# A two-layer decoder kernel: products of the identity put ahead of TensorE's expected waits

## The chip, the cores and the metric

The kernel runs on one core of one Trainium2 chip. The metric is the device time of one execution in microseconds (us). TensorE (PE, with its weight loads shown apart as PEld), VectorE (DVE), ScalarE (ACT), GpSimd (POOL) and SyncE (SP, which issues the DMAs) each work through a list of instructions of their own, in order, and wait for each other by semaphores.

## The reference

Two decoder layers on 8 sequences of 256 tokens with 512 features, all in float32. Each of the six stages adds its result to `x` and normalises:

```python
x = _layernorm(x + L0_attn(x))                 # power attention: 16 query, 8 key heads of 128, (qk)^2, gated decay, causal
x = _layernorm(x + L0_xattn(x, ctx, ctx))      # 16 heads of 32 over 256 context tokens, causal
x = _layernorm(x + L0_ffn(x))                  # router over 128 experts, top 4, eight shared bases, a shared expert
x = _layernorm(x + L1_attn(x))                 # 32 query heads of 16, 8 key heads, softmax, and a memory read
x = _layernorm(x + L1_xattn(x, ctx, mask))     # 16 heads of 32, queries and output in int8 steps
x = _layernorm(x + L1_ffn(x))                  # 8 experts, top 2
```

## The kernel before

**Work.** The 2048 tokens are held as four groups `g` of 512 tokens (two sequences each), all stages in one launch, stage after stage with overlaps. A float32 product is made of three products in the type fp32r, of a high and a low part of each operand (`mm3`, lines 665 to 667: high by high, high by low, low by high). ScalarE or GpSimd rounds a tile to its high part and VectorE subtracts to get the low part (`split_ps`, `split_w`; lines 635, 636, 640, 641). Results of TensorE go to banks of PSUM, which come from six rings of buffers: `w` and `v` of two, `z`, `y`, `mm` and `m2` of one (printed as `m`). `Ctx.bank` (line 624) gives out the next buffer of a ring; a step that asks for one cannot write it before the last reader of the buffer's former content is done.

**Steps.** The program is a list of some thousand small steps (`proj`, `scores`, `probs`, `turn` and so on), each with a planned time. `Plan.record` builds a draft of the whole program and notes which instructions each step issues. `listed` then plays the draft: it holds a time for each engine (`free`), a duration for every instruction by its form (`occupied`), the end of every instruction (`end`), and chooses again and again, from the steps whose planned time lies within a window, the one that could start first. The result is one order of steps. `Plan.run` issues the steps of the real program in this order, and ties the instructions of each engine to it. So each engine's list is fixed by the played times, not by what happens on the chip.

**Constants.** `Ctx` makes the 128x128 identity in two types, `ident` in float32 and `identr` in fp32r (lines 584 to 587). Transposes on TensorE use them; a transpose writes its bank as a product does.

**Names that the prediction uses.** At the start, `values.proj` of the first stage multiplies the first tokens (`axth`, `axtl`) by the value and gate weights (`wvh`, `wvl`); its inputs come by DMA and are split first. Near 1676 us, at the start of the fourth stage, `memory_out` multiplies the memory's two parts `mh`, `ml` with elements of the queries (`m<-mh,sh`), `scores` gives `w<-k,q`, VectorE takes maxima `nm` of them (line 2029), and the maxima are turned by products with `identr` (`max_turn`, line 1141, shown as `m<-identr,ns` on the helper's line 658). At 1987 us SP issues the loads of the fifth stage's constants, `bqc` among them (line 2211). Line 1021 turns sums of the first stage in 32x32 blocks, line 1673 (`counts`) multiplies the router's turned exponentials `et`, 128 columns of weights, with a table of only 10 columns, line 2329 turns probabilities of the fifth stage. The last microseconds are the last stage (`l1_ffn`) on the last tokens, step after step, with little beside it.

The run of the steps, before:

```python
for k, n in enumerate(order or range(len(steps))):
    m = len(ins)
    steps[n].f()
```

## Time and profile before

| | |
|---|---|
| time, median of 3 runs | 2397.93 us (2394.85 to 2399.33) |
| the profiled execution: its own time | 2399.13 us |
| its span, first to last instruction | 2397.4 us |
| mean granted clock of TensorE | 0.958 |
| TensorE products: busy, number | 2191.5 us, 12779 |
| TensorE weight loads: busy, number | 1670.0 us, 12800 |
| VectorE, ScalarE, GpSimd busy | 1506.3, 1094.0, 718.0 us |
| mean DMA rate | 95 GB/s |

Busy time of TensorE counts a product from its start to its modelled end. Products overlap, so the pace, from one start to the next, is shorter than a product's duration: a product of 128x512 takes some 395 ns and the next starts some 230 ns later. The granted clock is the share of its full clock that TensorE is given; in this profile it is 1 or 0.5. A row of the timeline gives start (us), time (us), engine, line, operation, what is written from what, weights, shape and type, number, and in brackets the idle time before it and what ended it. A row of the windows view gives the stretch, then the busy time and number of instructions of PE, PEld, DVE, ACT and POOL, the granted clock, the DMA share and GB/s.

### The profile page before, as it was taken

The numbers are of one execution on the slowest core, as the hardware profiler recorded it, in microseconds if no ns is written. First come the engines' busy times: TensorE is split into PE (matmuls) and PEld (weight loads), VectorE is DVE, ScalarE is ACT, GpSimd is POOL, SyncE is SP. The second block draws the span as 40 slices with busy tenths as digits, with TensorE's granted clock in tenths as the row PEclk, the third lists the DMA queues.
The fourth block names the chain that finished last, engine by engine and source line by source line (L and its number), as shares of the span: only waits on it lengthen the run. The fifth ranks groups of instructions, "written<-read, shape, count | busy, mean of one in ns | idle before, by whom it ended". The sixth has DMA issues, their size and how long they took to land.

```text
span 2397.4 us, 36873 instructions
## 1 busy us (share of the span) xinstructions
PE 2191.5 (91%) x12779; PEld 1670.0 (70%) x12800; DVE 1506.3 (63%) x3563; ACT 1094.0 (46%) x2697; POOL 718.0 (30%) x978
## 2 busy tenths in 40 slices
PE   7999999899999689988989999998999997878885
PEld 5888877688887567666778778886556564546663
DVE  5655666656556655555655554444777876778885
ACT  3443444444444565654211321112456554678884
POOL 3544444544444211111112201001112323523233
PEclk9999999999999899998999999999799998899997
DMA  4111122112112777752563201103454353765630
GB/s 141 49 40 45 58 76 71 45 57 80 40 36 84 201 215 206 205 167 80 56 147 119 69 33 53 36 1 98 84 93 87 79 92 78 172 157 141 177 80 36
DMA packets 146266, 226.83 MB, mean 95 GB/s; under 512 B 23680, under 2 KB 46848, under 8 KB 145824
## 3 DMA queue, kind: packets, MB, share of 16 engines
q1 hardware_dynamic: 146080, 224.48, 36.0%
q8 instruction: 102, 1.67, 0.3%
q14 instruction: 84, 0.69, 0.1%
HBM read 162.43 MB, written 57.79 MB: 92 GB/s over the span
## 4 chain that ended last, share of the span: by engine, by line
PE 65%; DVE 14%; DMA 7%; ACT 7%; issue 4%; POOL 2%; SPq 1%; ACTq 0%; DVEq 0%; POOLq 0%
PE v L665 5%; PE v L667 5%; PE v L666 5%; PE w L667 3%; PE w L665 3%; PE w L666 3%; PE mm L652 3%; PE mm L665 3%; PE mm L667 3%; PE mm L666 3%; PE z L665 2%; PE z L667 2%; PE z L666 2%; PE w L652 2%; PE z L652 2%
## 5 line engine op out<-in xcount | busy, mean ns | idle before, releaser
L1038 POOL TENSOR_TENSOR x<-x,ot 128x512 f32<-128x512 f32 x128 | 171.7, 1341 | 261.3 <-ACT ot L1037 199.8
L2029 DVE TENSOR_REDUCE nm<-w 128x2 f32<-128x512 f32 x256 | 166.1, 684 | 44.7 <-PE w L652 44.2
L2072 ACT ACTIVATE pr<-v 128x512 f32<-128x512 f32 x256 | 139.4, 595 | 81.3 <-PE v L652 80.7
L1701 ACT ACTIVATE sg<-w 128x512 f32<-128x512 f32 x64 | 38.1, 598 | 258.1 <-PE w L667 245.7
L1037 ACT ACTIVATE ot<-m,rn 128x512 f32<-128x512 f32 x128 | 88.0, 687 | 79.6 <-PE m L667 76.7
L2329 PE MATMUL w<-ident,pr 128*128 128x128 f32 x512 | 97.1, 297 | 27.3 <-ACT pr L2315 21.2
L1352 ACT ACTIVATE pr<-w,nm 128x128 f32<-128x128 f32 (+1 forms) x256 | 105.3, 425 | 27.9 <-DVE nm L1345 12.2
L1034 DVE SCALAR_TENSOR_TENSOR x<-mm,rn,x 128x512 f32<-128x512 f32 x128 | 95.3, 745 | 31.1 <-PE mm L667 30.1
L665 PE MATMUL w<-wgh,ph 128*128 128x512 f32 x256 | 102.1, 399 | 2.7 <-ACT sg L1701 2.7
L666 PE MATMUL w<-wgl,ph 128*128 128x512 f32 x256 | 101.2, 395 | 3.4 <-DVE wgl L1591 3.4
L2329 PEld LDWEIGHTS w<-ident,pr 128*128 128x128 f32 x512 | 61.0, 146 | 59.6 <-ACT pr L2315 54.9
L1345 DVE TENSOR_REDUCE nm<-w 128x1 f32<-128x128 f32 (+1 forms) x256 | 77.4, 347 | 39.5 <-PE w L1340 29.5
L667 PE MATMUL w<-wgh,pl 128*128 128x512 f32 x256 | 101.2, 395 | 0.0
L1410 POOL TENSOR_TENSOR x<-x,oo 128x256 f32<-128x256 f32 x32 | 24.7, 773 | 240.5 <-DVE oo L1406 240.5
L1590 POOL TENSOR_SCALAR wgh<-raw 128x512 fp32r<-128x512 f32 x40 | 26.1, 654 | 226.1 <-PE w L667 182.8
L1704 DVE TENSOR_TENSOR sg<-sg,v 128x512 f32<-128x512 f32 x42 | 28.8, 686 | 97.8 <-PE v L667 87.7
L636 DVE TENSOR_TENSOR yl<-y,yh 128x512 fp32r<-128x512 f32 x64 | 44.0, 688 | 70.3 <-ACT yh L635 70.3
L635 ACT ACTIVATE yh<-y 128x512 fp32r<-128x512 f32 x64 | 38.2, 597 | 108.8 <-PE y L667 106.1
L978 DVE TENSOR_TENSOR a<-w,se 128x512 f32<-128x512 f32 (+1 forms) x128 | 67.5, 549 | 21.6 <-PE w L667 19.0
L986 ACT ACTIVATE a<-a 128x768 f32<-128x768 f32 x64 | 54.0, 844 | 55.9 <-DVE a L978 55.9
L2115 POOL TENSOR_TENSOR x<-x,oo 128x256 f32<-128x256 f32 x32 | 23.4, 730 | 185.7 <-DVE oo L2104 148.3
L994 DVE TENSOR_TENSOR al<-a,ah 128x768 fp32r<-128x768 f32 x64 | 69.2, 1083 | 13.8 <-POOL ah L990 13.5
(609 smaller groups left out, 7227.2 us busy)
## 6 DMA issues: line engine op xcount, KB each, us to landing
q<-rs SPq DMA_DIRECT2D x90, 128.0 KB, 3.5
b_pair<-rs SPq DMA_DIRECT2D x42, 256.0 KB, 5.6
q<-rs SPq DMA_DIRECT2D x36, 256.0 KB, 4.2
k<-ke SPq DMA_DIRECT2D x36, 256.0 KB, 6.1
raw<-in_Wq_dram SPq DMA_DIRECT2D x32, 256.0 KB, 2.7
eb<-lg SPq DMA_DIRECT2D x32, 256.0 KB, 3.5
raw<-in_Wc_dram SPq DMA_DIRECT2D x32, 256.0 KB, 3.4
raw<-in_L_ffn_w_gate_dram SPq DMA_DIRECT2D x32, 256.0 KB, 4.0
```

Of the source, the lines that this page charges most:

```text
L652: ins = self.K.nc.tensor.matmul(*args, **kw)
L665: nc.tensor.matmul(ps, lh, rh, start=first, stop=False)
L666: nc.tensor.matmul(ps, lh, rl, start=False, stop=False)
L667: nc.tensor.matmul(ps, ll, rh, start=False, stop=last)
L1034: nc.vector.scalar_tensor_tensor(xt, st["o", r], c, xt, ALU.mult, ALU.add)
L1037: nc.scalar.activation(ot, st["o", r], AF.Copy, scale=c)
L1038: nc.gpsimd.tensor_tensor(xt, xt, ot, ALU.add)
L1345: nc.vector.tensor_reduce(m[:, t : t + 1], st["w", j][:, t, : (t + 1) * P], AX.X, ALU.max, negate=True)
L1352: nc.scalar.activation(p_[:, t * P : (2 * t + 1) * P], st["w", j][:, t, : (t + 1) * P], AF.Exp, bias=st["m", j][:, t : t + 1], accum_out=s ...
L2029: nc.vector.tensor_reduce(st["nm"][:, :, h], st["w", h], AX.X, ALU.max, negate=True)
L2072: nc.scalar.activation(st["p", h], st["w", h], AF.Exp, scale=SCALE)
L2329: ins = nc.tensor.transpose(v[:, sb, t * P : (t + 1) * P], st["p", j][:, t, sb * P : (sb + 1) * P], K.ident)
```

## The change

While `listed` plays the order, it now also looks at the first instruction of a step, where that is TensorE's and the step allots buffers. It takes the time from when TensorE is free to when the inputs that other engines make are ready (`gap`), subtracts `GAP` = 0.3 us, and notes a number of spare products for the step: `SHARE` = 0.55 of the rest, at 0.06 us for one, 60 at most. `Plan.run` hands the number to the step, and the first call of `bank` in it issues so many products of `identr` by `identr` into the buffer that it has just allotted. The step's own product then writes the same buffer with its accumulation started anew, so nothing of them is kept. Each of these products is an fp32r product of its own with its weight load: up to 128 weight columns (as many as the buffer has rows) and up to 128 columns streamed. The draft has no such products, so the played times, and with them the order of the steps, are the same as before.

```diff
--- before.py
+++ after.py
@@ -38,6 +38,7 @@
 ST_E, FI_E, DF_E = 0.0, 5.9, 3.9
 
 SB, W_A, W_B, W_C, WC, WDD = -3000, 26.2, 23.9, 17.8, -5, -30
+GAP, SHARE = 0.3, 0.55
 LP, LA, LV = 0.325, 0.235, 0.215
 SE, WINDOW, SLACK, QL_D, ML_D, W_D, QX_D, TP = -350.0, 35.5, 0.033, 20, 14, 22.8, 0, 10
 
@@ -292,6 +293,7 @@
 
     def __init__(self, tc):
         self.tc, self.steps, self.last, self.strict, self.step = tc, [], {}, 1e9, None
+        self.spare = 0
 
     def at(self, t, raw, f, *args):
         self.steps.append((t, raw, len(self.steps), partial(f, *args)))
@@ -309,11 +311,11 @@
             s.ins = list(ins[n:])
         return self
 
-    def run(self, order=None, first=0):
+    def run(self, order=None, first=0, spare={}):
         steps = self.sorted()
         ins = self.tc.nc.cur_bb.bb.instructions
         for k, n in enumerate(order or range(len(steps))):
-            m = len(ins)
+            m, self.spare = len(ins), spare.get(n, 0)
             steps[n].f()
             for i in ins[m:]:
                 e = str(i.engine)
@@ -397,7 +399,7 @@
     turns, rings, ready, floors = {}, {}, {}, {}
     left = {name: {s for s in u if s.n >= first} for name, u in users.items()}
     last_use = {}
-    order = list(range(first))
+    order, spare = list(range(first)), {}
     for s in steps[first:]:
         f = s.f.func
         stage, *_, name = f.__qualname__.split(".")
@@ -467,6 +469,9 @@
         stop = t
         for n, i, before in s.pred:
             e = str(i.engine).split(".")[-1]
+            if e == "PE" and i is s.pred[0][1] and s.allocs:
+                gap = max([0.0, *(end[j] for j in before)]) - free[e]
+                spare[s.n] = min(60, max(0, int((gap - GAP) * SHARE / 0.06)))
             occ, lat, mode_ = occupied(i, mode)
             t = max([free.get(e, 0.0), *(end[j] for j in before)])
             t = max([t, *(ready.get(v.bass_ap.tensor.name, 0.0) for v in i.outs if hasattr(v, "bass_ap"))])
@@ -489,7 +494,7 @@
         todo.remove(s)
         order.append(s.n)
     K.played = max(end.values())
-    return order, first
+    return order, first, spare
 
 
 class Phase:
@@ -627,7 +632,16 @@
             n = self.turns[tag] = self.turns.get(tag, -1) + 1
             tag = TURNS[tag][n % len(TURNS[tag])]
         self.bufs[tag] = RINGS[tag]
-        return self.noted(self.psum.tile(list(shape), dt, tag=tag, name=tag, bufs=RINGS[tag]), RINGS[tag], None, ring)
+        t = self.psum.tile(list(shape), dt, tag=tag, name=tag, bufs=RINGS[tag])
+
+        part = t
+        while len(part.shape) > 2:
+            part = part[:, 0]
+        n = min(P, part.shape[1])
+        for _ in range(self.plan.spare):
+            self.nc.tensor.matmul(f32(part[:, :n]), self.identr[:, : part.shape[0]], self.identr[:, :n], start=True, stop=True)
+        self.plan.spare = 0
+        return self.noted(t, RINGS[tag], None, ring)
 
     def split_ps(self, hi, lo, ps):
 
@@ -2613,8 +2627,7 @@
     same = [nc.dram_tensor(f"{'out' if a is args[-1] else 'in'}{i}", a.shape, a.dtype, kind="ExternalOutput" if a is args[-1] else "ExternalInput").ap() for i, a in enumerate(args)]
     draft = planned(ctx, tile.TileContext(nc).__enter__(), *same)
     draft.plan.record()
-    order, first = listed(draft, draft.start, draft.window, SLACK)
-    planned(ctx, tc, *args).plan.run(order, first)
+    planned(ctx, tc, *args).plan.run(*listed(draft, draft.start, draft.window, SLACK))
 
 
 def planned(ctx, tc, x, x_turned, ctx_2048, ctx_turned, mask, *weights_and_out):
```

## The prediction

> **What bounds the kernel now.** I read the page first (busy time, chain), then the windows view on the grid at which the clock changes, then the timeline at the places where products are added. The page:

> ```profile
> PE 2191.5 (91%) x12779; PEld 1670.0 (70%) x12800; DVE 1506.3 (63%) x3563; ACT 1094.0 (46%) x2697; POOL 718.0 (30%) x978
> ...
> PE 65%; DVE 14%; DMA 7%; ACT 7%; issue 4%; POOL 2%; SPq 1%; ACTq 0%; DVEq 0%; POOLq 0%
> ```

> TensorE sets the end: 65% of the chain, and idle for only 206 us of 2397.4. Time can come back in two ways: a wait ends sooner, or the products behind it run at the full clock. The mean granted clock is 0.958. The stretches at half clock all begin and end on one grid of 3.41 us, as in these windows (columns: window and length; busy us of PE, PEld, DVE, ACT, POOL with counts; granted clock; DMA share; GB/s):

> ```profile
> 2151.10:2154.51 3.41, 1.87 (x15) 1.37 (x14) 3.31 (x14) 3.20 (x11) 1.27 (x1) 1.00 0.23 72
> 2154.51:2157.93 3.42, 3.10 (x17) 2.14 (x19) 2.33 (x10) 3.26 (x11) 1.38 (x4) 0.50 0.08 16
> 2157.93:2161.34 3.41, 3.41 (x25) 2.37 (x18) 1.23 (x6) 2.26 (x9) 0.00 (x0) 0.50 0.96 219
> 2304.70:2308.11 3.41, 2.20 (x14) 1.62 (x15) 2.58 (x14) 3.41 (x12) 0.00 (x0) 1.00 0.90 217
> 2308.11:2311.53 3.42, 3.42 (x26) 1.82 (x23) 1.82 (x5) 2.28 (x10) 0.00 (x0) 0.50 0.00 0
> ```

> A window in which PE is busy for some 55 to 65% is followed by one at half clock, and a full window, or nearly, is needed to leave it. The start is at half clock too, whatever the clock column says there (it has no event before 14.36): products of 264 columns start 0.22 us apart until 14.4 and 0.12 us apart after:

> ```profile
> 13.72 0.42 PE L665 MATMUL z<-wvh,axth 128*128 128x264 f32 x1
> 13.94 0.42 PE L666 MATMUL z<-wvl,axth 128*128 128x264 f32 x1
> ...
> 14.74 0.28 PE L665 MATMUL v<-wvh,axth 128*128 128x264 f32 x1
> 14.86 0.28 PE L666 MATMUL v<-wvl,axth 128*128 128x264 f32 x1
> ```

> **What is added.** The order of steps is played on the draft, which has no extra products, so every engine keeps its order. Comparing the built programs, only TensorE's list differs: 401 products at 40 places. Their sizes are uneven: 60 at the start, 28 and 47 near 802 and 806 us, 15 near 820, 39 near 1678, 60 (16 weight columns) near 1989, 19 and 15 near 2371 and 2384; the other 32 places hold 1 to 9 each. TensorE works its list in order, so each one is free only as far as it lies in a wait that exists on the chip. The first of a place takes over the wait for its bank's last reader from the step's own product; no wait is new, and what is queued behind is TensorE's own list.

> **What one costs.** The code counts 0.06 us each. No row shows a 128-column fp32r product behind a full 128x128 load. Where only 10 columns follow such a load, eight products start within 0.81 us (1137.63 to 1138.44): about 0.11 us each, set by the load. With 128 columns streamed (0.12 x 128/264 = 0.06 us) the load still sets the pace, so I take 0.11 at full clock; bounds 0.06 and 0.12. At half clock the stream alone is 0.22 x 128/264 = 0.107, the lower bound. I take 0.215, because loads slow with the clock too. The short transposes of L1021 show it, four of them in 0.43 us (pace 0.06) against 0.63 (pace 0.11):

> ```profile
> 59.90 0.43 PE L1021 MATMUL m<-ident,nr 32*128 32x32 f32 x4
> 441.92 0.63 PE L1021 MATMUL m<-ident,nr 32*128 32x32 f32 x4
> ```

> [...]

> The same figures say what the products do to the clock: they stream 0.053 us in 0.11, so the array works half of the time. That is enough to lift a window that just failed (60% busy), and too little, I think, to leave half clock, which here took windows that were nearly full. [...] Here windows that were half busy lowered it, so I do not count on half-busy ones to raise it.

> **Place by place** (gap = idle time of PE before the next real product in the trace).

> Start: the first real product waits until 6.08, and the unit weights are ready at 1.62. 60 x 0.215 = 12.9 us, to 14.5: 8.5 late. PE idles 1.7 us between 6 and 12 and 2.5 between 18 and 22, which take up 4.2. Left **+4.3** (bounds: at 0.107 they end at 8.1 and nothing is left, 0; nothing taken up, +8.5). What runs late behind them is the value and query products on PE, then VectorE's splits.

> Near 802 to 824: 28, 47 and 15 products in gaps of 1.35, 4.29 and 1.57 us cost 3.1, 5.2 and 1.7 at full clock, 2.8 too much. PE waits here for weights and context by DMA, in windows of which 3.41 us is quite idle, so I take **0** (bounds -1.6, if the half-clock stretch at 823.32 goes; +5.8, if the 47 run at half clock).

> 1678: the player expected a long wait; the chip has almost none:

> ```profile
> 1677.56 0.63 PE L652 MATMUL mm<-dth,dql 128*128 128x512 f32 x1
> ...
> 1677.63 0.28 PEld L652 LDWEIGHTS m<-mh,sh 128*128 128x128 f32 x1 [0.16 <-POOL mh L640]
> 1677.99 0.42 PE L652 MATMUL m<-mh,sh 128*128 128x256 f32 x1
> ...
> 1680.75 0.58 PE L652 MATMUL w<-k,q 48*128 48x256 f32 x1 [1.86 <-DVE nm L2029]
> ```

> The clock is half (1676.65 to 1686.89), so 39 x 0.215 = 8.4, of which the 1.86 and 0.3 idle just behind take up 2.2: **+6.2** (bound at 0.107: +2.0). The score products `w<-k,q` and the maxima that VectorE takes from them run late.

> 1989 to 1995.7: only 16 weight columns are loaded, so the stream sets the pace: 60 x 0.107 = 6.4 in this gap:

> ```profile
> 1995.70 0.37 PE L658 MATMUL m<-identr,ns 128*16 128x128 f32 x2 [6.60 <-DVE ns L1134]
> ```

> **0** for the wait (+6.5 if they went at 0.215). They stream without pause, so the clock may be full from 1994.1 rather than 2000.9, where PE is busy 5.2 us: up to -2.6; VectorE is in the chain there, I take **-1.5**.

> 2064 to 2352: places with 1 to 8 products, all at full clock and 0.9 us at most in gaps of mostly 0.5 to 1.7: **0** for the waits, and so for the places with 1 to 9 products between 33 and 1062 and at 1670, 1693 and 2021, in gaps that they about fill. Eight of them lift the window of 2151.10 from 1.87 to about 2.7 us busy and six that of 2304.70 from 2.20 to about 2.9. The first pair of half-clock windows holds 6.5 us of PE work, the second window 3.4: up to -3.3 and -1.7. ScalarE is busy 3.2 of 3.4 us in the first, so I take **-1.6** and **-1.2**.

> The tail: 19 products at half clock cost 4.1 in a gap of 1.92, **+2.2** (0 at 0.107); 15 cost 1.65 in 1.11, **+0.5**; four at half clock cost 0.86 in 0.37, **+0.5**. Little work is left there to take this up.

> Sum: 4.3 + 6.2 - 1.5 - 1.6 - 1.2 + 2.2 + 0.5 + 0.5 = +9.4. Of the delay of 1678, later waits for DMAs that SP issues early (`q<-mx`, 4.1 us at 1770; `bqc`, issued at 1987.55) should take up some 2. **About +7.** The profiled execution took 2399.1 us (span 2397.4), 1.2 over the median of 2397.9: forecast 2406 for its like, 2405 for the median. With the bounds above this case gives -1 to +16; its own likely range is 2400 to 2412.

> **Rivals.** *Faster (0.14).* The products take 0.06 us as the code counts, 0.11 at half clock, and count as full work for the clock. Then 60 end near 6.3 at the start, 39 cost 4.2 - 2.2 = 2.0, the tail nothing. The clock gives 1.2 at the start (products from 12.0 to 14.4 at the full pace), 1.6 at 823, 2.6, 3.3 and 1.7 at the places above: 2.0 - 10.4 = -8, about 2390; half of it hidden behind VectorE, 2394. It decides if loads of unchanged weights cost less than 0.11. Against it: every product in the trace has its load, 12800 loads to 12779 products, those with unchanged weights too.

> *No change (0.26).* Loads do not slow at half clock: start 0, 1678 +2.0, tail +0.5, clock -4.3, so -2; or, between the two, about +2. 2396 to 2400.

> *It does less than it says:* 32 of the places hold under 10 products, and most half-clock stretches (393, 441, 775, 895, 1093, 1236, 1721, 1789, 1878) have no added product near them. That belongs to every case: they stay.

> **How the numbers follow.** About 0.2% (4.8 us) is what a measurement of this kernel can tell from no change: under 2393.1 faster, over 2402.7 slower. My case has 0.60 and mostly lies above that bound; what falls below it is set off by the upper part of the no-change case. The phase of the clock's grid against the kernel can move half-clock stretches by a few us either way, which widens each case. Range 2393 to 2413: it leaves out most of the faster rival and the far end of mine.

> **What would show it.** In the changed profile: the pace of the added products (0.11 and 0.215, or 0.06 and 0.11); the first real product at 14 to 15 us and still at half clock (or near 6.5 to 8); `m<-mh,sh` some 8 us behind `mm<-dth,dql` at 1678; no half-clock window behind 2151 and 2304. The forecast is wrong if the added products wake the clock at the start, or run at 0.06.

## The result, and the profile after

| | before | after |
|---|---|---|
| median time (lowest to highest of 12 executions each) | 2398.22 us (2385.67 to 2405.19) | 2407.53 us (2398.37 to 2415.08) |
| after by before | | 1.0042, 95% interval 1.0022 to 1.0062 |
| the profiled execution: its time, its span | 2399.13, 2397.4 us | 2402.09, 2400.3 us |
| mean granted clock in the profile | 0.958 | 0.968 |

The changed kernel is slower by 0.42%, some 10 us (5 to 15). The forecast was 2405 for the median, +7 us, in a range of 2393 to 2413. The profiled execution of after is one of its quickest, 5.4 us under its median: its trace shows what happens at a place, and it does not show the whole difference. For the whole I use the ratios of many executions.

In after, the helper `mm3` has lines 679 to 681, and the added products are line 642; other lines of the code behind it lie 14 further down. The page (busy time, chain):

```profile
PE 2223.0 (93%) x13180; PEld 1714.1 (71%) x13201; DVE 1508.4 (63%) x3563; ACT 1093.4 (46%) x2697; POOL 717.0 (30%) x978
...
PE 66%; DVE 15%; ACT 7%; DMA 7%; issue 3%; POOL 2%; SPq 1%; ACTq 0%; DVEq 0%; POOLq 0%
```

There are 401 more products and 401 more loads, TensorE is busy for 31.5 us more, and the span is 2.9 us longer. The other engines are as busy as before within 2.1 us (VectorE 1508.4 against 1506.3, ScalarE 1093.4 against 1094.0, GpSimd 717.0 against 718.0).

**The start**, timeline of TensorE. The last of the 60 and the first real products:

```profile
13.68 1.05 PE L642 MATMUL v<-identr 128*128 128x128 f32 x4
14.54 0.53 PE L679 MATMUL v<-wvh,axth 128*128 128x264 f32 x1
14.86 0.42 PE L680 MATMUL v<-wvl,axth 128*128 128x264 f32 x1
15.08 0.42 PE L681 MATMUL v<-wvh,axtl 128*128 128x264 f32 x1
```

The 60 ran from 1.68 to 14.5 us, 0.213 us apart, and did not wake the clock: the products behind them are 0.22 us apart until 18.6 us and 0.12 after.

To follow a delay through the kernel I compare the start of each VectorE instruction with the start of the same one in the trace of before (their list is the same in both); I call the difference its lateness. The kernels ran on several chips, and lateness is always against the one trace of before, so I read its steps at a place and not its level: between 1160 and 1300 us, where none of the kernels has an added product, it moves by -4.0 to +4.2 us from kernel to kernel. In after it is 4.7 us at 15 us, 3.5 at 45 and 3.5 at 790, and between 2.2 and 4.1 on the way.

**1678**, timeline of TensorE (1684 in this trace):

```profile
1683.55 0.63 PE L666 MATMUL mm<-dth,dql 128*128 128x512 f32 x1
1683.97 4.70 PE L642 MATMUL m<-identr 128*128 128x128 f32 x39
1688.51 0.33 PE L666 MATMUL m<-mh,sh 128*128 128x256 f32 x1
...
1689.01 0.50 PE L666 MATMUL w<-k,q 48*128 48x256 f32 x4
```

The product `m<-mh,sh` starts 4.96 us behind `mm<-dth,dql`; before it was 0.43. The scores `w<-k,q` start 5.46 behind it, before 3.19: 2.3 us later. The clock was half until 1684.45 only, so nearly all 39 went 0.112 us apart.

**1989**, timelines of VectorE and TensorE (1999 in this trace; L1992 is `memory_add`, L1978 in before):

```profile
1998.75 0.17 DVE L2230 TENSOR_SCALAR bqc<-bqc 128x4 f32<-128x4 f32 x1 [8.37 <-DMA bqc<-in_L_xattn_bq_dram]
...
1999.09 0.35 DVE L1992 SCALAR_TENSOR_TENSOR x<-m,rd,x 128x128 f32<-128x128 f32 x1
1999.36 0.17 DVE L1147 TENSOR_SCALAR ns<-nm 128x16 fp32r<-128x16 f32 x1
```

```profile
1999.59 6.24 PE L642 MATMUL m<-identr 128*16 128x128 f32 x60 [7.01 <-DVE ns L1147]
2005.67 0.28 PE L672 MATMUL m<-identr,ns 128*16 128x128 f32 x2
```

TensorE idles for 7.01 us first, and only then come the 60. They need no `ns`; what they need is their bank. In the built program the semaphore value that the first of them waits for is that of `memory_add`, which reads the bank's former content, while the real product waits for a value two instructions further on, at the end of `ns`. Both stand behind the scaling of `bqc` on VectorE, and that waits 8.37 us for its DMA. So the wait that the products were to fill holds them back too, and their 6.1 us come after it.

**2154 and 2308**, windows of after (columns as in the prediction; the first three lie on its own grid, the last two start 0.23 us ahead of it):

```profile
2155.50:2158.91 3.41, 2.38 (x16) 1.79 (x16) 2.96 (x12) 3.20 (x9) 1.33 (x3) 1.00 0.00 0
2158.91:2162.33 3.42, 3.42 (x25) 1.93 (x23) 1.94 (x9) 3.11 (x11) 0.43 (x2) 0.50 0.41 114
2162.33:2165.74 3.41, 3.25 (x26) 2.46 (x23) 2.83 (x12) 2.50 (x9) 0.00 (x0) 1.00 1.07 227
...
2305.44:2308.86 3.42, 2.50 (x20) 2.02 (x18) 2.58 (x14) 3.14 (x10) 0.00 (x0) 1.00 0.79 199
2308.86:2312.27 3.41, 3.25 (x34) 2.31 (x35) 2.40 (x8) 3.41 (x14) 0.00 (x0) 1.00 0.15 46
```

Of the pair of half-clock windows behind 2151 one is left, and the one behind 2304 is gone. The window of 2155.50 holds the eight products and is 70% busy, and the next is at half clock all the same, while the window of 2305.44, 73% busy, is followed by full clock: busy time does not set the two apart (experiments on the start, below). Eight of the kernel's own products (`v<-k,q` and `w<-ident,pr`, four each), which stood in the window of 2151.10 before, now fall into the one ahead. One trace does not show that the added products did any of this. Behind 2151, five of the six kernels below that hold no products there have one half-clock window left and one has two; of the five others that hold the change's products there, four have none and one has one. Behind 2304 four of those six have none either, and none of those five has one.

**The tail**, timeline of TensorE:

```profile
2372.84 4.32 PE L642 MATMUL m<-identr 128*128 128x128 f32 x19 [0.78 <-DVE x L2560]
2376.96 0.65 PE L707 MATMUL m<-ident,x 128*128 128x128 f32 x2
```

They go 0.213 us apart and the real product starts 4.1 us behind the first of them. Lateness rises from 0.7 to 2.9 us here, and it is 2.9 at the end.

### The profile page after: what moved, and what is told of

Its sections match the earlier page's. It is cut to its first block, busy times and chain, and to the rows that moved or that the text cites. A ratio compares the mean times of both kernels' runs of the same rounds, so it can differ in the third digit from the quotient of the medians.

```text
span 2400.3 us, 37654 instructions
## 1 busy us (share of the span) xinstructions
PE 2223.0 (93%) x13180; PEld 1714.1 (71%) x13201; DVE 1508.4 (63%) x3563; ACT 1093.4 (46%) x2697; POOL 717.0 (30%) x978
## 4 chain that ended last, share of the span: by engine, by line
PE 66%; DVE 15%; ACT 7%; DMA 7%; issue 3%; POOL 2%; SPq 1%; ACTq 0%; DVEq 0%; POOLq 0%
PE v L679 5%; PE v L681 5%; PE v L680 5%; PE w L679 3%; PE w L681 3%; PE w L680 3%; PE mm L666 3%; PE mm L679 3%; PE mm L681 2%; PE mm L680 2%; PE z L679 2%; PE z L681 2%; PE z L680 2%; DVE nm L2043 2%; PE v L666 2%
## 5 line engine op out<-in xcount | busy, mean ns | idle before, releaser
L1008 DVE TENSOR_TENSOR al<-a,ah 128x768 fp32r<-128x768 f32 x64 | 70.7, 1106 | 13.7 <-POOL ah L1004 13.5
```

## The experiments

My theory after the result: each place costs what its products outlast the wait, at 0.112 us each at full clock and 0.213 at half, and gives back what the clock gains. The rivals: that delays are taken up by the DMA waits anyway, that products ahead of the queue cost something everywhere, and, for the places singled out, the prediction's own view. The kernels are the change with another table of products (number of the step: how many). Times are ratios to executions of before on the same chip. The diffs are shortened: the kernels write out whole tables, and `...` stands for what is left out.

| kernel | ratio to before, 95% interval | us |
|---|---|---|
| start only (60) | 1.0018, 1.0001 to 1.0034 | +4.3 |
| the start only, 30 with 512 columns | one profiled execution, no ratio | |
| 802 to 826 only (93) | 1.0019, 1.0006 to 1.0032 | +4.5 |
| 1678 and the tail only (81) | 1.0006, 0.9992 to 1.0020 | +1.4 |
| 1989 only (60) | 1.0016, 1.0001 to 1.0031 | +3.8 |
| 1989 only, into a free bank | 1.0003, 0.9986 to 1.0019 | +0.7 |
| the change without start, 1678, 1989, 19 and 15 | 0.9993, 0.9975 to 1.0011 | -1.7 |
| the change with 16 weight columns | 1.0000, 0.9990 to 1.0011 | 0.0 |
| mended | 0.9986, 0.9971 to 1.0001 | -3.4 |
| mended, 16 weight columns | 0.9992, 0.9981 to 1.0004 | -1.9 |
| chosen by the trace, 512 columns | 0.9995, 0.9984 to 1.0006 | -1.2 |
| mended and trimmed | 0.9997, 0.9983 to 1.0010 | -0.7 |

**The start alone.**

```diff
-    return order, first, spare
+    return order, first, {25: 60}
```

> Of the added products only the 60 at the start are kept. Theory (each place costs what its products outlast the wait, at 0.112 us each at full and 0.213 at half clock): they run from 1.7 to 14.3 us, the first real product starts at 14.5, still at half clock, and everything from 45 to 790 us runs 3.5 us later than before; in the changed kernel this lateness had shrunk to about 1 us behind 802. If the clock gained there is what took it back, it stays at 3 to 3.5 here and the time is +3 us (0 to +6 by the clock's phase). Rival (the wait for weights and context by DMA near 802 takes the lateness up, whatever stands ahead): it shrinks to under 1.5 us behind 802 here as well, and the time is within 1.5 us of before.

The first real product starts at 14.54, still at half clock. Lateness is 4.5 us at 15 us and between 2.0 and 3.5 from 35 us to 790. The time is up by 4.3 us (0.2 to 8.1). On the way the lateness did shrink, to 1.4 us at 1000, as in the rival, although no product is left at 802. So the trace does not show that the clock near 823 took it back, and the time does not show that it was taken back: one trace mixes it with stretches at half clock that lie elsewhere from trace to trace (near 1680 us half clock ends at 1686.89 in before and at 1684.45 in after).

**Without the five.**

```diff
+    for n in (25, 4378, 5751, 7505, 7535):
+        spare.pop(n)
     return order, first, spare
```

> The change without five of its 40 places: the 60 at the start, the 39 at 1678, the 60 at 1989 and the 19 and 15 of the tail are left out, 208 products at 35 places stay. Theory (the cost lies in these five, +3.5, +2.7, +3.5, +2.2 and +0.5, and the others pay for themselves by the clock at 823, 2154 and 2308): -3 us against before (-6 to +1), and 6 to 12 us less than the changed kernel. Rival (products ahead of the queue cost something at every place): +1 to +4 us against before.

0.9993 against 1.0042 for the whole change: with these five places its loss goes. That it would be faster than before is not shown, the interval holds 1.

**1989, in its own bank and in a free one.**

```diff
-    return order, first, spare
+    return order, first, {5751: 60}
```

> Only the 60 products near 1989 are kept. Theory (their bank's last reader is VectorE's memory_add, which stands in VectorE's list behind the scaling of bqc, and that waits for its DMA): TensorE idles some 6 to 7 us, then the 60 run for about 6 us, the real product starts 6 us after it could; 3 to 6 us of lateness behind it, half clock until about 2005, time +3 us (+1 to +6). The prediction's own view: the 60 run inside the wait, nothing late, the clock full some 7 us sooner, time 0 to -1.5.

The 60 start at 1992.74, 0.15 us behind the end of `memory_add`, after an idle time of 6.12. The real product starts at 1998.83. Lateness goes from -2.7 at 1996 to +0.9 at 2005, 3.6 us; half clock lasts from 1984.8 to 1998.5, as long as before. +3.8 us (0.2 to 7.4).

```diff
         part = t
+        if self.plan.spare:
+            part = self.psum.tile([P, 512], F32, tag="y", name="y", bufs=RINGS["y"])[: t.shape[0]]
```

> The same 60 products at the same place of TensorE's list, but written to a bank of the ring y, whose last reader is long done. Theory (it is the bank's release, not the products, that costs): they start when TensorE falls idle, run 6.0 to 6.4 us inside the wait of 6.6 to 7, the real product is late by 0.5 us at most; as they stream without pause the half-clock stretch there ends one or two windows of 3.41 us sooner than before; time 0 to -2.5 us, and 3 to 6 us less than with the 60 in their own bank. Rival (60 products of 16 weight columns at half clock outlast the wait by themselves, or the bank does not matter): late by 3 to 6 us as in the other kernel.

The timeline of TensorE (lines here lie two further down again):

```profile
1987.23 4.51 PE L644 MATMUL y<-identr 128*16 128x128 f32 x60
1993.38 0.28 PE L674 MATMUL m<-identr,ns 128*16 128x128 f32 x2 [1.64 <-DVE ns L1150]
```

Now the 60 run inside the wait, with 1.64 us of it to spare, and the real product is late by nothing. The clock, half from 1985.5, is full from 1988.9: 3.4 us of half clock instead of 13.7. Same products, same place in the list, real product at 1998.83 there and at 1993.38 here: it was the bank. But the gain in time did not come. Two new half-clock stretches (2002.6 and 2012.8, 10.2 us together) followed, and lateness, -3.7 at 2005, was -0.2 at 2020 and -4.0 at 2050. From 1996 to 2050 it falls by 1.7 us here, by 0.1 to 1.7 in the four other kernels whose products there go to the free bank, and by 1.2 to 4.3 in the five kernels with no products there; with the 60 in their own bank it rises by 1.7 in the kernel above and 1.0 in after, and falls by 0.2 in the kernel with 16 weight columns below. So the traces show the cost of the own bank, 3.2 to 3.6 us at the place in these three, and they show no gain of the free bank over having no products. In time the two kernels of this pair differ by 1.2 us in their medians, less than 12 executions each can tell apart.

**What a product loads and streams.** First, all products with 16 weight columns:

```diff
-            self.nc.tensor.matmul(f32(part[:, :n]), self.identr[:, : part.shape[0]], ...
+            self.nc.tensor.matmul(f32(part[:16, :n]), self.identr[:, :16], ...
```

> All 401 products stay at their places, but each loads only 16 weight columns instead of up to 128 and still streams 128 columns. Theory (the load sets the pace of the added products, 0.112 us at full and 0.213 at half clock; without it the stream does, 0.057 and 0.107; and an array that streams without pause wakes the clock where one that streams half of the time does not): the 60 at the start end by 7.5 to 8.2 us instead of 14.4, the first real products behind them start 0.12 us apart (full clock) instead of 0.22, lateness 0 to 1 us at 60 us; the 39 at 1678 cost 2.2 to 4.2 us, the 60 at 1989 are unchanged (+3.5 to +6), the 19 of the tail cost 1 us less or more; time -1 us against before (-5 to +3). Rival (every product costs the same, whatever it loads): the first real product at 14.5 us as in the changed kernel, and its time.

```profile
1.67 6.30 PE L642 MATMUL v<-identr 128*16 128x128 f32 x60 [1.67 <-DVE identr L592]
7.82 0.34 PE L679 MATMUL v<-wvh,axth 128*128 128x264 f32 x1
7.99 0.28 PE L680 MATMUL v<-wvl,axth 128*128 128x264 f32 x1
```

The pace is 0.107 us at half clock and 0.06 from 7.5 us on, where the clock rose; lateness at 60 us is -0.7. At 1678 the 39 take 3.0 us instead of 4.5. At 1989, where 16 columns were loaded before too, lateness still rises by 3.2. The kernel's time is that of before (-2.4 to +2.6 us): the load of 128 columns made about all the difference between +10 us and nothing.

Then only the start, with full loads and 512 streamed columns:

```diff
+            # n = 512; identr is read a = n // P times over
-            ... self.identr[:, : part.shape[0]], self.identr[:, :n], ...
+            ... self.identr[:, : part.shape[0]], self.identr[:, None, : n // a].to_broadcast([P, a, n // a]), ...
```

> Only the start, with 30 products of 128 weight columns that stream 512 columns each (identr read four times over). Theory (what wakes the clock is the share of time in which columns are streamed, whatever is loaded): they start 0.43 us apart at first and 0.23 after the clock has risen, between 5 and 9 us; the first real product starts at 9.8 to 12 us, and the ones behind it 0.12 us apart. Rival (added products of the identity do not wake the clock at the start at all, their kind or the cold start keeps it low): 0.43 us apart to the end, first real product at 14.5, then 0.22 us apart.

```profile
1.68 8.55 PE L645 MATMUL v<-identr 128*128 128x512 f32 x30 [1.68 <-DVE identr L592]
10.06 0.28 PE L682 MATMUL v<-wvh,axth 128*128 128x264 f32 x1
10.18 0.28 PE L683 MATMUL v<-wvl,axth 128*128 128x264 f32 x1
```

The pace changes at 4.7 us from 0.427 to 0.23 us, and the real products go 0.12 us apart from the first. The same load, with 128 columns behind it, went along with half clock for 12.6 us; with 512 the clock is full 3.0 us behind the first product. The load is the same in the two kernels, so what tells them apart is the columns streamed. My reading is that these are counted window by window on the grid on which the clock changes. Its step is 3.413 us: in the traces of before and after every half-clock stretch but the last, which the end of the kernel cuts, lasts 1 to 5 times that. Its place against the kernel differs between traces: the clock rises at 14.36 us in before and at 18.74 in after, so an edge lies at 0.7 in the one and at 1.7 in the other. In this trace a window runs from 1.3 to 4.7 and is streamed for some 89%: the clock rises at its end. In the kernel with 16 columns it runs from 0.7 to 4.1 and is streamed for some 70%: half clock goes on behind it, and the clock rises only at 7.5, after a full one. The one execution took 2381.84 us, where the 23 of before on that chip took 2386.27 to 2394.43; a single execution does not make a ratio.

The windows of all 14 traces bear this out, with a broad middle. For each I estimated the share of it in which columns are streamed, at 0.12 us for 264 columns at full clock, as measured, and twice that at half (measured: 0.22), with overlapping products counted once. Of the windows at half clock, all 185 with over 85% were followed by full clock, none of the 181 with under 45%, and 212 of the 374 between. Of those at full clock, 252 of the 289 with under 30% were followed by half clock, and none of the 7158 with over 55%. So in these traces less kept the clock up than woke it: of the full-clock windows with 50 to 55%, 418 of 420 were followed by full clock. The 39 at 1678 in after show it: they stream about half of the time (0.06 of 0.112 us) and fill the window from 1684.45 to 1687.86, and the next one is still at full clock.

**1678 and the tail.**

```diff
-    return order, first, spare
+    return order, first, {4378: 39, 7505: 19, 7535: 15, 7540: 4, 7546: 4}
```

> Only the 39 products at 1678 and the 19, 15, 4 and 4 of the tail are kept. Theory: the 39 start as soon as TensorE reaches them, wherever the clock stands, 0.112 us apart at full and 0.213 at half clock, 4.4 to 8.4 us; 2.2 of it lie in waits just behind, so VectorE's maxima run 2.5 to 6.2 us later there, and part of that is gone by 1900, because the full window lets the clock rise; the tail adds 2 to 3 us (19 at 0.213 = 4.1 in a gap of 1.9). Time +3 us (0 to +6). The prediction's own numbers: +6.2 and +3.2, 2 absorbed, +7. Rival (they lie in waits): 0.

The 39 take 5.0 us, mostly at full clock again; lateness rises from -4.3 to -1.6 there and is back at -3.7 by 1710. The 19 of the tail add 1.6; from 2369 to the end lateness rises by 0.5. +1.4 us (-1.9 to +4.8): less than the prediction's 7.

**802 to 826.**

```diff
-    return order, first, spare
+    return order, first, {2263: 28, 2256: 47, 2273: 1, 2305: 15, 2329: 2}
```

> Only the 28, 47, 1, 15 and 2 products between 802 and 826 are kept. Theory (they outlast their waits a little, 28 x 0.112 = 3.1 in 1.35 and 47 x 0.112 = 5.3 in 4.29, and give it back by windows at full clock around 806 to 826): 1 to 2.5 us later at 805 to 815, half-clock stretches between 800 and 830 shorter by one or two windows of 3.41 us, 0 to -2 us behind 830; time within 2 us of before (the prediction's 0). Rival (the gain of the kernel without the five costly places comes from here): -2 to -5 us.

+4.5 us (1.4 to 7.7), a miss for theory and rival. The timelines of TensorE, before and then this kernel, which runs 1.24 us ahead here:

```profile
802.37 0.50 PE L665 MATMUL mm<-cth,ekh 128*128 128x512 f32 x1 [1.35 <-ACT ekh L727]
...
804.74 0.50 PE L667 MATMUL mm<-cth,ekl 128*128 128x512 f32 x1 [1.63 <-DVE ekl L732]
...
810.44 0.77 PE L1331 MATMUL w<-b_pair 96*128 96x256 f32 x2 [4.29 <-DMA b_pair<-bk]
```

```profile
802.67 0.45 PE L679 MATMUL mm<-cth,ekh 128*128 128x512 f32 x1
...
803.50 0.50 PE L681 MATMUL mm<-cth,ekl 128*128 128x512 f32 x1 [0.15 <-DVE ekl L746]
...
809.97 0.45 PE L1345 MATMUL w<-b_pair 96*128 96x256 f32 x2
```

The first product is 1.5 us late and the next wait takes all of it; behind the 47 it is 0.8 late. Then ScalarE waits for the next weights (`raw` of `wkT`) for 12.5 us, before 11.3, though their load was issued 1.21 us ahead of before, like everything else here. Lateness rises by 3.5 us from 790 to 840; in the kernels with no products here it rises by 0.5 to 2.4 as well, and in the others that hold them it moves by -0.5 to +3.0. So the trace puts under 1 us down to these products, and some 1 to 3 to a load that landed late or to chance. Where the measured +4.5 comes from stays open. It also sits badly with the kernel without the five, which holds the same 93 products and measured -1.7: its other 115 would have to gain some 6 us, or one of the two figures lies at the edge of its interval.

The clock did answer here, in every trace. Half clock between 805 and 835 us (times of before) lasts 17.0 to 23.9 us in the seven traces without products at 802 to 826, before among them, and 3.4 to 10.2 us in the seven with them, and the stretch at 823 is gone in all seven. The kernel with these products alone was no faster for it.

**Versions made to be better.** Mended, with the change's own products:

```diff
+    for n in (4378, 7478, 7505, 7535, 7540, 7546):
+        spare.pop(n)
+    spare[25] = 30                       # and 5751 writes to the ring y
```

> The change mended at its costly places, with its own products: 30 instead of 60 at the start (30 x 0.213 = 6.4 us, they end at 8.1, 2 late, which waits until 20 us take up), those at 1989 written to the free bank of the ring y, none at 1678 and none from 2365 on. Theory (cost only where the products outlast a wait, gains by the clock at 823, 1989, 2154, 2308): -3 us against before (-7 to +1), 10 us less than the change. Rival (the clock's stretches only move to other places): 0, -1 to +2.

```diff
+    for n in (4378,):
+        spare.pop(n)
+    spare[25] = 40                       # all with 16 weight columns, and 5751 writes to the ring y
```

> As the change, but all products load 16 weight columns, 40 at the start (40 x 0.107 = 4.3 us, inside the wait that ends at 6.08), those at 1989 in the free bank of the ring y, none at 1678; the tail's stay (they cost 1.2 us at most with 16 columns). Theory (streaming without pause, they raise the clock more surely than the half-busy ones and cost half): -4 us against before (-9 to 0). Rival (as above): 0.

Of the first, the 30 end at 8.1 as worked out, and lateness is 0.2 at 20 us; its products at 1989 run inside their wait (1995.81 to 1999.4, the real one at 2003.71). Neither differs from before by more than the measurement can tell; the first comes nearest, 0.9986 (0.9971 to 1.0001), and is clearly better than the change's 1.0042. Over its 12 executions the mean clock is 0.9654, against 0.9577 for 29 of before on that chip.

Other places, read from the trace, with 512 columns (79 products at 21 places; the expectation miscounts them as 68 at 20):

```diff
-    return order, first, spare
+    return order, first, {25: 12, 47: 5, 82: 1, 1095: 3, 1217: 1, 2581: 2, 4303: 5, 4372: 2, 4593: 1, 4818: 1, 5751: 13, 5943: 17, ...}
```

> Other products at other places: 512 columns streamed for each load (so the array streams all the time that they take, 0.23 us each), and only 68 of them at 20 places where the trace of before, not the played order, shows a wait ahead of or inside a half-clock stretch: 12 at the start, 5 at 20 us, 3 at 390, 2 at 885, 5 at 1650, 2 at 1688, 13 at 1989 in the free bank, 17 at 2036, 4 at 2323, and 1 to 3 at 33, 456, 1721, 1789, 2154 to 2307. Theory (a window is kept at full clock by the share of it in which columns are streamed): granted clock 0.97 or more, half-clock stretches at 393, 1690, 2036 and 2325 gone or shorter, 5 to 15 us less than before, 0.5 to 1.1 us later at 1650 and 2323. Rival (stretches only move, or the delays at these places eat the gain): within 3 us of before.

A miss. The clock went from 0.9577 to 0.9616 only. The half-clock stretches at 2036 and 2325 were gone, others stood at 394, 1688, 2077 and 2101, and lateness rose by 1.2 us between 21 and 27, 1.4 at 465 and 1.2 at 1650. The rival had it: stretches move, and delays eat the rest.

Trimmed, the mended kernel with 232 products at 31 places:

```diff
+    spare.update({25: 18, 2263: 20, 2256: 36, 2305: 11, 2329: 1, 6403: 1})
+    for n in (82, 4403, 7393):
+        spare.pop(n)
```

> The mended change with fewer products where the trace still showed them outlasting the wait: 18 at the start (18 x 0.213 = 3.8 us, inside the wait that ends at 6.08), 20, 36 and 11 instead of 28, 47 and 15 at 802 to 822, none at 33, 1694 and 2351, one at 824 and 2139; those at 1989 in the free bank of the ring y; the others as in the change; 232 products at 31 places. Theory: -5 us against before (-9 to -1), a little better than the mended kernel (ratio 0.9986). Rival (what is gained is one or two windows of the clock, which come and go with the phase): 0 to -3.

0.9997 (0.9983 to 1.0010), a miss for the theory: no gain over the mended one, and no sign that the few tenths that products outlast their waits were what it lacked.

## Why the prediction was right

Its direction and its sum held, +7 forecast and +10 (5 to 15) measured; the terms did so only in part. By their kernels, the parts are 4.3 (start) + 1.4 (1678, tail) + 3.8 (1989) - 1.7 (all others; the tail's last two places, of four products each, are counted twice) = +7.8. Each of these is uncertain by some 3 to 4 us, so that they meet the whole is no sharp test; that the loss lies in the five places is shown by the kernel without them.

- **The price** of 0.11 and 0.215 us was right: 0.112 and 0.213. With 16 weight columns it is 0.06 and 0.107, so the load sets it. The trace of before had the price already, in float32: where two transposes of the form `128*128 128x128` follow each other, they start 0.109 us apart at full clock and 0.213 at half (medians of 1061 and 80 pairs). The prediction asked for fp32r alone. Its 0.053 us of streaming is half of the 0.107 it worked out for half clock, an estimate; with 16 weight columns 0.06 was measured at full clock, so the products stream about half of their 0.112 us, as it said.
- **The start**, +4.3: measured +4.3 (0.2 to 8.1) by its kernel, 3.5 in the trace of after. The 60 ended at 14.5 as worked out and left the clock low, as the prediction argued from an array that works half of the time (0.107 of each 0.213 us).
- **802 to 824**, 0 (-1.6 to +5.8): the trace of its kernel agrees within 1 us, the time of that kernel says +4.5. Inside the bounds, not explained. The stretch at 823 went, as the lower bound supposed, and no time came of it.
- **1678**, +6.2: mis-sized. `m<-mh,sh` was 5.0 us behind `mm<-dth,dql`, where the prediction had 8, and the scores were 2.3 late. The term took the half-clock stretch of the trace of before (until 1686.89) as given. The grid lay elsewhere: the clock rose 0.5 us behind the first of the 39 in after (1684.45) and 1.7 behind it in the kernel with 1678 and the tail alone, so most of them went at the full pace in both traces that hold them with full loads. In after the window that ended there, from 1681.03, was filled by the real products ahead of them. Where the grid lies differs from trace to trace.
- **1989**, 0 for the wait and -1.5 by the clock: this step failed. It measured +3.8 (0.2 to 7.4) alone, and +3.5 of lateness in the trace of after. The prediction said in general that the first product of a place takes over the wait for its bank's last reader, and then gave this place the whole gap of 6.60 us without looking who that reader was. It stood behind the same `bqc` wait. The free bank shows the mechanism.
- **2064 to 2352**: lateness in after falls from 5.2 us at 2050 to 0.7 at 2360, so no cost of the waits is seen, as said. In after one of two windows at half clock behind 2151 is gone, and the one behind 2304; most kernels without products there lost as much, so it is not shown that the terms -1.6 and -1.2 were earned. The reading under them, that a window 55 to 65% busy is followed by half clock, held for its two windows and not in general: of 331 full-clock windows of the 14 traces that are 50 to 70% busy, 75 were. Nor was a nearly full window always needed to leave half clock: of the 374 streamed for 45 to 85%, 212 were followed by full clock. The 35 places that stay without the five, those at 802 among them, come to -1.7 us (-6.0 to +2.6).
- **The tail**: the 19 cost 2.2 us in after, as worked out; the others under 1, and none of that is left at the end. With 1678 they measured +1.4 (-1.9 to +4.8) where the terms made 7.4 (6.2 + 3.2 less 2).

So the sum was met by luck: one term was some 5 us too low (1989) and one some 4 too high (1678). The price, the start and the tail were right by their mechanism. Of the rivals, the faster one fell with the price and the sleeping clock at the start; no change fell with the pace at half clock. What the faster one hoped for, that added products wake the clock, was seen at the start with products that stream all the time: at 4.7 us with 512 columns, at 7.5 with 16 weight columns.

## What to carry to other kernels

A filler takes over its bank's wait: before counting a gap as free, find that bank's last reader and what that reader stands behind, and write to a bank that has long been read. At 1989 the own bank cost 3.2 to 3.6 us of lateness and the free one none. Work added to wake TensorE's clock did so here where it streamed columns with hardly a pause (all 185 half-clock windows streamed for over 85% were followed by full clock, none of the 181 under 45%): products that only filled their load slots, 128 columns behind a load of 128, cost 0.213 us each and did not wake it in 12.6 us. To keep a full clock up, streaming for half of a window was nearly always enough (418 of the 420 full-clock windows with 50 to 55%). But the half clock spared at 802 to 826 (3.4 to 10.2 us of it where the kernels without products there have 17.0 to 23.9), where TensorE waits for DMAs, saved no time that the runs show. And one trace is not enough for differences of a few us: lateness moves by -4.0 to +4.2 us between 1160 and 1300 us, where no kernel has an added product, and the clock's windows lie elsewhere from trace to trace. Read the mechanism at the place from a trace, and the total from many executions.
